# Where layer 1's own product is made, and which block layer 0 takes first

## The chip, the cores and the metric

The kernel runs on one core of one Trainium2 chip. The metric is the device time of one execution in microseconds. A core has five engines that run side by side and wait for one another by semaphores: TensorE (PE, matrix products and transposes, with its weight loads shown apart as PEld), VectorE (DVE), ScalarE (ACT), GpSimd (POOL) and SyncE (SP). In this kernel GpSimd issues the gathers and SyncE most plain transfers; sixteen DMA engines move the data.

## The reference

Four graph layers on N = 3327 nodes with D = 512 features. Each is `x = layernorm(x + layer(x, adj))`. `adj` is sparse (about 0.24% of the pairs times a weight that falls with the node number, so the first rows have by far the most neighbours).

```python
# layer 0: attention with 8 heads of 64
Wh = einsum('nd,hdo->hno', x, W);  f1, f2 = Wh.a1, Wh.a2
e = where(adj > 0, leaky_relu(f1[:, :, None] + f2[:, None, :]), -9e15)
x = layernorm(x + elu(softmax(e) @ Wh))
# layer 1: mean of the neighbours
agg = (adj > 0) @ x / max(deg, 1)
out = concat([x @ W_self + b_self, agg @ W_nb + b_nb]) @ W_comb + b_comb
x = layernorm(x + relu(out))
# layer 2: mean of the first 64 neighbours, its own weights
x = layernorm(x + leaky_relu(x @ W_line.T + b) + leaky_relu(mean64 @ W_nb.T + b))
# layer 3: attention with 4 heads of 128
```

Layer 1's output before the relu is linear in x. The kernel therefore makes two fused weights, `wx = W_self @ W_comb[:D]` and `wn = W_nb @ W_comb[D:]`, so that a node needs `x @ wx` ("own part", or self part, called z) and the mean over its neighbours of `x @ wn`.

## The kernel before

Nodes are worked on in NB = 26 blocks of 128. For each block an edge list is made first (on VectorE, from the adjacency rows); it says which table rows to gather. A chunk is 128 edges. Block 0 has three lists of 14 chunks; blocks 1 to 4 have 19, 15, 13 and 11 chunks, and later blocks from 10 down to 5. Up to four chunks form a group (one "item").

The edge lists are made by a generator, `structure`, that is advanced a step at a time between other work. The order of blocks is given here:

```python
LATE0 = 16
FIRST = 3
order = [*range(1, FIRST + 1), 0, *range(FIRST + 1, NB)]
...
def structure(big, mid, ps, m0):
    ...
    ms = masks(order[0], fetch(order[0]))       # ScalarE: adj -> 0/1; block 0's mask goes to m0
    yield None
    for k, b in enumerate(order):
        ab = fetch(order[k + 1]) if k + 1 < NB else None
        ...                                      # the list of block b
        yield k
```

Layer 0 first projects all blocks (`x @ W` into a table in HBM), then takes the items in the order of the blocks. The end of a block makes the new x, transposes it, multiplies by wn and stores the result as a row table for layer 1; for blocks below NB - LATE0 it also multiplies by wx:

```python
def layer0_end(b, acc):
    yield
    x1 = xres[b]
    e, mv, rs = yield from g0.summed(fin, acc, x1)
    scaled_by_act(x1, e, fin, mv, rs)
    xt = transposed(fin, ps, x1)                 # four 128x128 transposes, one copy
    yield
    tb = fin.tile([P, D], F32, name="tb", bufs=2)
    t3 = fin.tile([P, 3, D], BF16, name="t3", bufs=2)
    for _ in pieces(t3, tb, times(ps, xt, wn)):  # three bf16 pieces
        pass
    store(t1_d, b, t3.rearrange("p s d -> p (s d)"), 2)
    if b >= NB - LATE0:
        return
    yield
    zb = fin.tile([P, D], F32, name="tb", bufs=2)
    nc.scalar.copy(zb, times(ps, xt, wx))
    store(z1_d, b, zb)
...
for k, item in enumerate(groups(pools[0], order)):
    while ready < order.index(item[0]):
        more()                                   # one step of the lists
    work.add(g0.group(item, pools, accs, layer0))
    work.step()
    more(2 if k % 8 == 0 else 1)
```

Layer 1 takes block 0 densely (26 chunks in seven items, the adjacency row as weights) and the others through gathers of table rows into a ring. With each of the first LATE0 items one block's own part is made that layer 0 left out, with a transpose of its own:

```python
early = list(range(NB - LATE0, NB))
def self_part(b):
    yield
    xt = transposed(xts, ps, xres[b])            # the second transpose of x
    yield
    zb = fin.tile([P, D], F32, name="tb")
    nc.scalar.copy(zb, times(ps, xt, wx))
    store(z1_d, b, zb)
...
for items in (first_items(), groups(ring, range(1, NB))):
    for item in items:
        b, at = item[0], item[4]
        if at == 0:
            xin[b] = fin.tile([P, D], F32, name="zb", bufs=3)
            load(xin[b], z1_d, b)
        work.add(mean_group(item, t1_d, row0, lambda b, acc: ends.add(layer1_end(b, acc))))
        if early:
            ends.add(self_part(early.pop(0)))
        both()                                   # one step of all that is under way
```

`mean_group` gathers, makes a selection matrix, and adds up with three bf16 products per chunk. `layer1_end` adds z and the bias, normalises, transposes the new x and multiplies by layer 2's two weights (wn2 and wl2). The ring of layer 1 holds 15 + 4 chunks.

One more part is touched. From block 0's mask `m0` two transposed masks are made, one for all neighbours (row0) and one for the first 64 (near0). `near` has the place of the running count:

```python
zeros16 = lent(3 * D, BF16)
nc.gpsimd.memset(zeros16, 0.0)
...
so_far = lent(NP, I16)
nc.gpsimd.memset(rows[:, free:], 0.0)            # the rest of the ring
near = so_far.bitcast(BF16)
nc.vector.tensor_tensor_scan(so_far, m0, m0, 0.0, ALU.add, ALU.bypass)
for o in (row0, near0):
    if o is near0:
        nc.vector.scalar_tensor_tensor(near, so_far, KEEP, m0, ALU.is_le, ALU.mult)
    ...                                          # 26 transposes of m0 or near
```

Of the kernel before, what the change touches and what calls it, by code (L numbers as in the profile page):

```python
# [9 lines left out]
BF16 = mybir.dt.bfloat16  # L10
# [527 lines left out]
DENSE0 = 12  # L538
DENSE = 2
AHEAD = 2  # L540
LATE0 = 16

FIRST = 3
RING = 22 * 528
MORE = 3072
RANGE = 60.0
# [75 lines left out]
def sparse_path(ctx, tc, flag_i, x, adj, l0_w, l0_a1, l0_a2, l1_w_self, l1_b_self, l1_w_nb, l1_b_nb,  # L622
# [30 lines left out]
    dram = ctx.enter_context(tc.tile_pool(name="s_dram", bufs=1, space=DRAM))  # L653
    keep = pool_in(ctx, "s_keep")

    order = [*range(1, FIRST + 1), 0, *range(FIRST + 1, NB)]
    lists = []
    for b in range(NB):
        parts = HEAVY if b == 0 else ((0, SEGMENTS[b], CAPS[b], SLOTS[b], SEGMENTS[b], 1),)
# [168 lines left out]
    def structure(big, mid, ps, m0):  # L828
# [6 lines left out]
        def fetch(b):  # L835
            ab = abs_[b % len(abs_)]
            for s in range(2):
                w = min(HW, N - s * HW)
                if b == NB - 1:
                    nc.gpsimd.memset(ab[s][96:P, :], 0)  # L840
                for p0, p1 in rows_of(b):
                    nc.sync.dma_start(ab[s][p0:p1, :w], adj[b * P + p0:b * P + p1, s * HW:s * HW + w])
            return ab

        def masks(b, ab):
            ms = []
            for s in range(2):
                m = m0[:, s * HW:(s + 1) * HW] if b == 0 else big.tile([P, HW], BF16, name="m", bufs=2)
                nc.scalar.activation(m, ab[s], AF.Sign, accum_out=half[:, s, b:b + 1])  # L849
                ms.append(m)  # L850
            return ms

        ms = masks(order[0], fetch(order[0]))
        yield None
        for k, b in enumerate(order):
            ab = fetch(order[k + 1]) if k + 1 < NB else None
            val = big.tile([P, NP], U16, name="val")
            for s in range(2):
                nc.vector.tensor_mul(val[:, s * HW:(s + 1) * HW], ms[s], code[:, s * HW:(s + 1) * HW])
# [5 lines left out]
            for q, l in enumerate(lists[b]):  # L865
# [7 lines left out]
                for s in range(len(cuts) - 1):  # L873
                    seg = val[:, cuts[s]:cuts[s + 1]]
                    for r in range(rounds):
                        top = cand[:, s * rounds + r, :]
                        nc.vector.max(out=top, in_=seg)  # L877
                        if r + 1 < rounds:
                            nc.vector.match_replace(out=seg, in_to_replace=top, in_values=seg, imm_value=0.0)
                    if s == (len(cuts) - 1) // 2:  # L880
                        if q == 0 and ab is not None:
                            ms = masks(order[k + 1], ab)
                        yield None
                cf = cand.rearrange("p s e -> p (s e)")
                sl = mid.tile([P, K + 1], F32, name="sl")
# [34 lines left out]
                for c0 in range(0, L, G):  # L920
# [19 lines left out]
                    with nc.allow_low_precision(reason="whole numbers below 4096"):  # L940
                        nc.vector.tensor_reduce(l.idx[:, c0:c0 + g], eq, AX.X, ALU.add)
                    nc.vector.scalar_tensor_tensor(l.dst[:, c0:c0 + g], l.idx[:, c0:c0 + g], 0.0, v[:, :, 0],
                                                   ALU.is_gt, ALU.mult)
            yield k

    def groups(ring, blocks=range(NB)):

# [312 lines left out]
    with ExitStack() as pro:  # L1260
        wp = pool_in(pro, "l0pw", side="right")
        xp = pool_in(pro, "l0px", 2, side="right")
        ps3 = pool_in(pro, "l0pp3", 3, space=PSUM)
        ps2 = pool_in(pro, "l0pp2", 2, space=PSUM)
        ps1 = pool_in(pro, "l0pp1", 1, space=PSUM)

        ps = Banks(ps1, po=ps3, tr=ps2)
        banks = Banks(ps1, pv=ps2)
        m0 = lent(NP, BF16)
        made = structure(big, mid, banks, m0)  # L1270
        w0 = lent(DC * (D + 3 * H0)).rearrange("p (c s o) -> p c s o", c=DC, s=2)
        for c in range(DC):
            for s in range(2):
                nc.sync.dma_start(by_heads(w0, c, H0)[:, s],
                                  l0_w[s * H0 // 2:(s + 1) * H0 // 2, c * P:(c + 1) * P, :].rearrange("h p o -> p h o"))
        a0 = lent(2 * D).rearrange("p (s h o) -> p s h o", s=2, h=H0)
        for s, src in enumerate((l0_a1, l0_a2)):
            nc.sync.dma_start(a0[:, s].rearrange("p h o -> p (h o)"), row(src, H0 * OUT0))
        g0 = Gat("g0", t0_d, H0, OUT0, w0, 0)
        next(made)  # L1280
        score_weights(w0, xp, a0, H0, OUT0)

        def projection(b):
            load(xres[b], x, b)
            yield
            xt = transposed(xp, ps, xres[b], g0.xsum, b)
            yield
            pw = g0.products(ps, xt)
            yield
            g0.write(b, xp, pw)  # L1290

        def fused_weights():

            wc = lent(2 * DC * D).rearrange("p (c o) -> p c o", o=D)
            nc.sync.dma_start(wc, l1_w_comb.rearrange("(c p) o -> p c o", p=P))
            bc = wp.tile([P, D], F32, name="bcomb")
            nc.sync.dma_start(bc, row(l1_b_comb, D))
            bs = wp.tile([P, 2 * DC, 1], F32, name="bs")
            with nc.allow_non_contiguous_dma(reason="two small biases"):
                nc.sync.dma_start(bs[:, :DC, 0], l1_b_self.rearrange("(c p) -> p c", p=P))  # L1300
                nc.sync.dma_start(bs[:, DC:, 0], l1_b_nb.rearrange("(c p) -> p c", p=P))
            for s, (src, o) in enumerate(((l1_w_self, wx), (l1_w_nb, wn))):
                for i in range(DC):
                    raw = xp.tile([P, D], F32, name="raw")
                    nc.sync.dma_start(raw, src[i * P:(i + 1) * P, :])
                    yield
                    rt = transposed(xp, ps, raw)
                    yield
                    po = times(ps, rt, wc[:, s * DC:(s + 1) * DC, :])
                    nc.scalar.copy(o[:, i, :], po)  # L1310
            pb = ps.tile([P, D], F32, name="po")
            for k in range(2 * DC):
                bb = wp.tile([P, P], F32, name="bb", bufs=2)
                nc.vector.tensor_copy(bb, bs[:, k].to_broadcast([P, P]))
                nc.tensor.matmul(pb, bb, wc[:, k, :], start=k == 0, stop=k == 2 * DC - 1)
            nc.vector.tensor_add(bias1, pb, bc)

        def first_rows():

            zeros16 = lent(3 * D, BF16)  # L1320
            nc.gpsimd.memset(zeros16, 0.0)
            zero = zeros16[0:1, :]
            for r in range(2):
                nc.sync.dma_start(t1_d[r:r + 1, :], zero)
                nc.sync.dma_start(t2_d[r:r + 1, :], zero)
            so_far = lent(NP, I16)
            nc.gpsimd.memset(rows[:, free:], 0.0)
            near = so_far.bitcast(BF16)
            nc.vector.tensor_tensor_scan(so_far, m0, m0, 0.0, ALU.add, ALU.bypass)
            for o in (row0, near0):  # L1330
                if o is near0:
                    nc.vector.scalar_tensor_tensor(near, so_far, KEEP, m0, ALU.is_le, ALU.mult)
                for c0 in range(0, NB, 8):
                    g = min(8, NB - c0)
                    yield
                    pt = banks.tile([P, 8, P], BF16, name="lp")
                    for c in range(g):
                        src = m0 if o is row0 else near
                        nc.tensor.transpose(pt[:, c, :], src[:, (c0 + c) * P:(c0 + c + 1) * P], ident16)
                    nc.scalar.activation(o[:, c0:c0 + g, :], pt[:, :g, :], AF.Identity, saturate=False)  # L1340

        ready, whole = -1, True

        def more(n=1):
            nonlocal ready, whole
            for k in range(n):
                b = next(made, None)
                whole = b is not None or ready == NB - 1
                ready = ready if b is None else b

        fused = Stages()
        for t in range(NB):
            work.add(projection(t))
            work.step()
            more(3)
            if t == 4:
                fused.add(fused_weights())
            if t == 10:
                fused.add(first_rows())
            fused.step()  # L1360
        work.drain(more)
        fused.drain(more)
        g0.finish(xp, ps)
        while not whole:
            more()
# [42 lines left out]
                nc.scalar.copy(o[:, :, k * P:(k + 1) * P], pt)  # L1408

    w2lay = ExitStack()  # L1410
    for k, item in enumerate(groups(pools[0], order)):
        while ready < order.index(item[0]):
            more()
        work.add(g0.group(item, pools, accs, layer0))
        work.step()
        more(2 if k % 8 == 0 else 1)
        if ready == NB - 1 and wn2 is None:
            listlay.close()
            extra = pool_in(ctx, "s_more").tile([P, MORE], F32, name="gx")
            sp = pool_in(ctx, "s_sel", 3)  # L1420
            wp = pool_in(w2lay, "l2w")
            wn2 = wp.tile([P, DC, D], F32, name="wn2")
            wl2 = wp.tile([P, DC, D], F32, name="wl2")
            rawp = pool_in(lay, "l2raw", 2)
            work.add(transposed_weights())
# [322 lines left out]
```

## Time and profile before

| what | value |
|---|---|
| time, median of 3 runs | 1705.97 us (1705.8 to 1707.22) |
| profiled execution | 1704.1 us |
| PE, VectorE, ScalarE, GpSimd busy | 89%, 73%, 45%, 54% |
| moved by DMA | 410.17 MB, mean 241 GB/s |

Engines are busy side by side, so shares don't add up. A line of groups in the profile has the engine, the operation, its tiles with shapes, how often it occurs, busy time and mean of one, and then the idle time just before it with what ended that. A fp32 product of a block with a 512x512 weight is eight matmul records (four chunks of the weight, two records each); the transposes of a block are four. In time order the execution is: projection and first lists (to about 220 us), layer 0's blocks (to about 670), layer 1 (to about 1095), layer 2 (to about 1380), layer 3.

The matmuls of these parts on the page:

| group | records | busy us | mean ns |
|---|---|---|---|
| product with wx | 208 | 94.3 | 596 |
| product with wn or wn2 | 416 | 192.9 | 607 |
| transposes of x | 520 | 79.9 | 277 |
| layer 0's weighted sum | 1656 | 413.7 | 399 |

### The profile page before, as it was taken

The numbers are of one execution on the slowest core, as the hardware profiler recorded it, in microseconds if no ns is written. First come the engines' busy times: TensorE is split into PE (matmuls) and PEld (weight loads), VectorE is DVE, ScalarE is ACT, GpSimd is POOL, SyncE is SP. The second block draws the span as 40 slices with busy tenths as digits, with TensorE's granted clock in tenths as the row PEclk, the third lists the DMA queues.
The fourth block names the chain that finished last, engine by engine and source line by source line (L and its number), as shares of the span: only waits on it lengthen the run. The fifth ranks groups of instructions, "written<-read, shape, count | busy, mean of one in ns | idle before, by whom it ended". The sixth has DMA issues, their size and how long they took to land.

```text
span 1704.1 us, 25362 instructions
## 1 busy us (share of the span) xinstructions
PE 1523.7 (89%) x7947; PEld 981.5 (58%) x7947; DVE 1243.4 (73%) x3256; ACT 773.2 (45%) x2411; POOL 911.9 (54%) x1008
## 2 busy tenths in 40 slices
PE   5798958999999999999999999889989866998774
PEld 4565746777666664444444444446555545877653
DVE  8999988999998973124777884565434468798986
ACT  6557855667776764111111121122223222566664
POOL 2000067777666613646776552477777552677770
PEclk9999979999999999999999999999999987999997
DMA  8623687998775637978998776589999664677772
GB/s 300 233 100 107 207 288 237 313 309 266 258 231 176 179 90 282 317 237 272 341 328 296 246 241 241 204 279 317 318 312 322 234 227 157 189 230 224 227 220 74
DMA packets 121982, 410.17 MB, mean 241 GB/s; under 512 B 24768, under 2 KB 26304, under 8 KB 121838
## 3 DMA queue, kind: packets, MB, share of 16 engines
q0 software_dynamic: 69584, 286.13, 52.8%
q1 hardware_dynamic: 52254, 122.32, 20.4%
q8 instruction: 65, 1.06, 0.3%
q14 instruction: 79, 0.65, 0.1%
HBM read 360.34 MB, written 48.04 MB: 240 GB/s over the span
## 4 chain that ended last, share of the span: by engine, by line
PE 61%; DVE 16%; DMA 11%; ACT 6%; issue 3%; POOL 2%; SPq 0%; DVEq 0%; ACTq 0%; POOLq 0%
PE po L765 20%; PE acc L1196 15%; PE acc L1474 14%; DMA gt<-t_d,idx 7%; PE po L998 6%; PE pt L750 2%; DVE cand L877 2%; DVE gt L1188 2%; DMA gx<-t_d,idx 2%; POOL gt L966 2%; PE pg L1168 2%; DMA gd<-t_d 1%; DVE cand L891 1%; DVE sl L889 1%; ACT h L1213 1%
## 5 line engine op out<-in xcount | busy, mean ns | idle before, releaser
L966 POOL DMA_INDIRECT gt<-t_d,idx x739 | 742.1, 1004 | 578.9 <-DVE some L893 210.6
L1196 PE MATMUL acc<-gt,sel 128*128 128x264 f32 (+4 forms) x1656 | 413.7, 399 | 27.1 <-issue 20.1
L1196 PEld LDWEIGHTS acc<-gt,sel 128*128 128x128 f32 (+2 forms) x1656 | 311.4, 195 | 97.8 <-issue 42.9
L1188 DVE TENSOR_TENSOR gt<-gt,pg 128x1536 f32<-128x1536 f32 (+2 forms) x128 | 238.6, 1864 | 6.3 <-ACT gt L1181 2.9
L765 PE MATMUL po<-wn,xt 128*128 128x512 f32 x416 | 192.9, 607 | 3.8 <-ACT xt L753 3.8
L1474 PE MATMUL acc<-gt,sall 128*128 128x512 bf16 x489 | 117.3, 379 | 17.6 <-DMA gt<-t_d,idx 14.3
L765 PEld LDWEIGHTS po<-wn,xt 128*128 128x128 f32 x416 | 77.2, 193 | 89.4 <-issue 78.4
L966 POOL DMA_INDIRECT gx<-t_d,idx x107 | 107.6, 1006 | 38.6 <-issue 14.9
L877 DVE MAX8 cand<-val 128x8 f32<-128x832 uint16 (+38 forms) x259 | 125.7, 522 | 0.0
L1474 PEld LDWEIGHTS <-sall 128*128 128x128 fp8e4 x603 | 58.3, 97 | 98.4 <-issue 35.3
L1474 PE MATMUL acc<-gt,sel 128*128 128x512 bf16 (+3 forms) x486 | 113.3, 379 | 0.0
L998 PE MATMUL po<-gt,xt 128*128 128x268 f32 x416 | 106.0, 400 | 2.0 <-ACT xt L757 1.7
L1474 PEld LDWEIGHTS <-sel 128*128 128x128 bf16 (+3 forms) x603 | 57.9, 98 | 80.0 <-issue 22.7
L1156 ACT ACTIVATE far<-place,nmid 128x384 int16<-128x384 int16 (+3 forms) x137 | 86.9, 637 | 37.5 <-DVE ds L1160 34.5
L753 ACT COPY xt<-pt 128x512 f32<-128x512 f32 x86 | 50.8, 591 | 113.3 <-PE pt L750 113.2
L998 PE MATMUL po<-w,xt 128*128 128x262 f32 x416 | 96.2, 384 | 1.6 <-ACT xt L757 1.6
L765 PE MATMUL po<-wl,xt 128*128 128x512 f32 x208 | 94.0, 594 | 2.9 <-ACT xt L753 2.9
L765 PE MATMUL po<-wx,xt 128*128 128x512 f32 x208 | 94.3, 596 | 1.3 <-ACT xt L753 1.2
L750 PE MATMUL pt<-s_ident,xres 128*128 128x128 f32 x520 | 79.9, 277 | 17.4 <-DMA xres<-in_x_dram 16.6
L750 PEld LDWEIGHTS pt<-s_ident,xres 128*128 128x128 f32 x520 | 63.8, 143 | 46.2 <-issue 31.2
L1009 ACT COPY tg<-po 128x264 f32<-128x264 f32 (+1 forms) x104 | 39.9, 392 | 110.8 <-PE po L998 108.9
L849 ACT ACTIVATE m<-ab 128x1664 bf16<-128x1664 int32 x50 | 80.4, 1607 | 20.5 <-DMA ab<-in_adj_dram 15.6
(273 smaller groups left out, 2555.4 us busy)
## 6 DMA issues: line engine op xcount, KB each, us to landing
ab<-in_adj_dram SPq DMA_DIRECT2D x25, 832.0 KB
ab<-in_adj_dram SPq DMA_DIRECT2D x25, 831.5 KB
t_d<-t SPq DMA_DIRECT2D x50, 384.0 KB
gt<-t_d POOLq DMA_DIRECT2D x38, 384.0 KB, 7.8
gt<-t_d,idx POOLq DMA_INDIRECT x739, 4.8
t_d<-tg SPq DMA_DIRECT2D x25, 264.0 KB
t_d<-tg SPq DMA_DIRECT2D x25, 260.0 KB
gd<-t_d SPq DMA_DIRECT2D x25, 260.0 KB
```

The lines of the kernel that those rows point to most:

```text
L750: nc.tensor.transpose(pt[:, c, :], src[:, c * P:(c + 1) * P], ident)
L753: nc.scalar.copy(xt, pt)
L765: nc.tensor.matmul(po, xt[:, c, :], w[:, c], start=c == 0, stop=c == DC - 1)
L849: nc.scalar.activation(m, ab[s], AF.Sign, accum_out=half[:, s, b:b + 1])
L877: nc.vector.max(out=top, in_=seg)
L966: nc.gpsimd.indirect_dma_start(out=t[:m, c, :], out_offset=None, in_=table[:, :], in_offset=bass.IndirectOffsetOnAxis(ap=l.idx[:m, c0 + c: ...
L998: nc.tensor.matmul(pw[s], xt[:, c, :], self.w[:, c, s, :], start=c == 0, stop=c == DC - 1)
L1009: nc.scalar.copy(tb[:, s * hh:(s + 1) * hh, :], by_head[:, :, 1:])
L1156: nc.scalar.activation(far[:, :g * P], place[:, c0 * P:(c0 + g) * P], AF.Abs, bias=l.nmid, scale=2.0)
L1188: nc.vector.tensor_mul(Gc[:, :, :OUT], Gc[:, :, :OUT], w[:, :g].rearrange("p c (h o) -> p (c h) o", o=1).to_broadcast([P, g * H, OUT]))
L1196: nc.tensor.matmul(accs[b][s], S[:m, c, :], G[:m, c, s * hh * M:(s + 1) * hh * M], start=at + c == 0, stop=at + c == chunks_of[b] - 1)
L1474: nc.tensor.matmul(accs[b], S[:m, c, :], G[:m, c, k * D:(k + 1) * D], start=at + c + k == 0, stop=k == 2 and at + c == n - 1)
```

## The change

It does three things. LATE0 becomes 4, so the own part of all blocks but the last four is made at the end of layer 0's blocks, from the transposed x that is there, and twelve second transposes in layer 1 go. Layer 0 takes the blocks in plain order, block 0 first. And the mask for the first 64 neighbours is made in place of `m0`, without the memset of the ring's rest.

```diff
-LATE0 = 16
-
-FIRST = 3
+LATE0 = 4
...
-    order = [*range(1, FIRST + 1), 0, *range(FIRST + 1, NB)]
...
-        ms = masks(order[0], fetch(order[0]))
+        ms = masks(0, fetch(0))
         yield None
-        for k, b in enumerate(order):
-            ab = fetch(order[k + 1]) if k + 1 < NB else None
+        for b in range(NB):
+            ab = fetch(b + 1) if b + 1 < NB else None
...
-            yield k
+            yield b
...
-            zeros16 = lent(3 * D, BF16)
-            nc.gpsimd.memset(zeros16, 0.0)
-            zero = zeros16[0:1, :]
+            zero = lent(3 * D, BF16)[0:1, :]
+            nc.gpsimd.memset(zero, 0.0)
...
-            nc.gpsimd.memset(rows[:, free:], 0.0)
-            near = so_far.bitcast(BF16)
...
-                    nc.vector.scalar_tensor_tensor(near, so_far, KEEP, m0, ALU.is_le, ALU.mult)
+                    nc.vector.scalar_tensor_tensor(m0, so_far, KEEP, m0, ALU.is_le, ALU.mult)
...
-    for k, item in enumerate(groups(pools[0], order)):
-        while ready < order.index(item[0]):
+    for k, item in enumerate(groups(pools[0])):
+        b = item[0]
+        while ready < b:
             more()
```

More of the change, by code (lines that the diff above doesn't have):

```diff
@@ L881, in structure @@
                         if q == 0 and ab is not None:
-                            ms = masks(order[k + 1], ab)
+                            ms = masks(b + 1, ab)
                         yield None
@@ L1337, in first_rows @@
                     for c in range(g):
-                        src = m0 if o is row0 else near
-                        nc.tensor.transpose(pt[:, c, :], src[:, (c0 + c) * P:(c0 + c + 1) * P], ident16)
+                        nc.tensor.transpose(pt[:, c, :], m0[:, (c0 + c) * P:(c0 + c + 1) * P], ident16)
                     nc.scalar.activation(o[:, c0:c0 + g, :], pt[:, :g, :], AF.Identity, saturate=False)
```

## The prediction

> **What bounds the kernel now.** I read the page's engine totals and its 40 slices first, to see whether one engine bounds everything. None does by its total, but the matmul engine is full from the seventh slice on, after VectorE has been full:
>
> ```profile
> PE 1523.7 (89%) x7947; PEld 981.5 (58%) x7947; DVE 1243.4 (73%) x3256; ACT 773.2 (45%) x2411; POOL 911.9 (54%) x1008
> ...
> PE   5798958999999999999999999889989866998774
> ...
> DVE  8999988999998973124777884565434468798986
> ```
>
> So the change has to be read by stage. The table of stretches, cut where the timeline changes character, gives each engine's busy time (PE, weight loads, DVE, ACT, POOL), the granted clock, the DMA share and GB/s:
>
> ```profile
> 0.00:220.00 220.00, 179.33 (x1041) 128.48 (x1041) 206.02 (x778) 144.59 (x507) 9.12 (x27) 0.97 0.57 192
> 220.00:270.00 50.00, 30.66 (x264) 25.24 (x265) 38.58 (x100) 27.56 (x73) 37.97 (x39) 0.77 0.89 297
> 270.00:640.00 370.00, 364.12 (x2278) 258.77 (x2276) 336.99 (x843) 256.95 (x741) 229.73 (x253) 0.99 0.71 225
> 640.00:674.00 34.00, 30.66 (x115) 16.75 (x114) 12.05 (x28) 17.57 (x41) 13.10 (x26) 1.00 0.85 311
> 674.00:780.00 106.00, 106.00 (x381) 51.20 (x380) 20.27 (x39) 20.17 (x37) 52.48 (x57) 1.00 0.78 262
> 780.00:920.00 140.00, 140.00 (x508) 64.03 (x507) 99.23 (x200) 23.21 (x46) 105.36 (x102) 1.00 0.94 324
> 920.00:1015.00 95.00, 95.00 (x331) 42.61 (x330) 76.48 (x161) 19.19 (x37) 48.44 (x48) 1.00 0.75 240
> ```
>
> The reader is to see five things. To 220 us (projection of x, edge lists) VectorE is busy 206 of 220. From 220 to 270 (the first gathers of layer 0) nothing is full and PE works 31 of 50. From 270 to 640 (rest of layer 0's blocks) PE has 364 of 370, VectorE 337. From 674 to 1015 (layer 1) PE is busy all the time. Within it, DMA is nearly full only from 780 to 920.
>
> Busy PE could still hide waits, so I went on to the timeline of PE just after 674 us. Columns are start, length, engine, line, operation:
>
> ```profile
> 677.38 3.60 PE L765 MATMUL po<-wx,xt 128*128 128x512 f32 x8
> 680.82 0.60 PE L750 MATMUL pt<-s_ident,xres 128*128 128x128 f32 x4
> 681.25 2.75 PE L1474 MATMUL acc<-gt,row 128*128 128x512 bf16 x12
> 683.84 3.60 PE L765 MATMUL po<-wx,xt 128*128 128x512 f32 x8
> ```
>
> Each starts where the one before stops delivering. From start to start: a product with wx takes 680.82-677.38 = 3.44 us, four transposes 681.25-680.82 = 0.43 us, four chunks of layer 1's neighbour sum 683.84-681.25 = 2.59 us (0.65 a chunk). These pitches, not the busy times, are what I charge. Layer 1's first 106 us are thus one self part (3.87 us) plus one group, again and again, sixteen times; the product of a self part stays in layer 1 for blocks 10 to 25.
>
> Last, who waits on that stretch. The groups of 674 to 780 us show GpSimd's gathers waiting for PE, not the reverse:
>
> ```profile
> L966 POOL DMA_INDIRECT gt<-t_d,idx x40 | 38.6, 966 | 36.8 <-PE acc L1474 30.4 <-issue 6.1 <-DMA gt<-t_d 0.3
> ```
>
> 40 gathers there lost 30.4 us because their ring slots were still being read. Where they run free, the timeline of GpSimd gives the pitch:
>
> ```profile
> 787.01 0.95 POOL L966 DMA_INDIRECT gt<-t_d,idx  x1 [0.30 <-issue]
> 788.27 0.95 POOL L966 DMA_INDIRECT gt<-t_d,idx  x1 [0.31 <-issue]
> ```
>
> That is 0.95 busy and 0.30 of issue: 1.25 us a gather.
>
> **What the Trainium skill says.** "Perfetto Trace Analysis", section "Identifying the Most-Contended Engine", says that matmul busy share misjudges the distance to the limit because matmuls are pipelined. The trace agrees: the page has 596 ns busy for one wx matmul, eight of them would be 4.8 us, and the pitch is 3.44. The same page, "Optimization Strategy", says a kernel with several regimes can gain by interleaving them. The old kernel does this in layer 1: self parts, which need no table, lie beside the front of the gathers. "TensorE: Matmul & The Clock Gate", section "Part 4: PE-mode transpose", says a transpose goes to PSUM and must be copied out, and gives about 275 ns in a kernel's context. The page shows 277 ns busy, and 591 ns for ScalarE's copy of four; but four follow one another in 0.43 us, so the second transpose of x is cheap. "DMA: Bandwidth & Descriptors", section "Where 436 GB/s comes from", puts HBM's limit for one core at about 358 GB/s. Here a share of 0.94 goes with 324 GB/s, so about 324/0.94 = 345 is all there is.
>
> **The change part by part.**
>
> First, LATE0 goes from 16 to 4. Twelve blocks (10 to 21) get their own product at the end of their layer-0 block, from the transposed x that is still there. Removed in layer 1: 12 x (3.44 + 0.43) = 46.4 us of PE, and 12 copies of 0.59 us on ScalarE, which lie beside PE and count nothing. Added in layer 0: 12 x 3.44 = 41.3 us. The difference of the work alone is 12 x 0.43 = 5.2 us. Both places lie where PE is the bound, so each term counts almost fully.
>
> Not quite fully in layer 0: between 552 and 604 us PE shows waits of 0.38, 1.09, 0.83 and 2.46 us for VectorE or ScalarE, 4.8 together. Blocks 10 to 21 end about there, so I take 4 us back: layer 0 gets 37 us longer. The products share one PSUM bank with the lists' small matmuls, but the old kernel does the same for blocks 0 to 9 and shows no wait on PE from 290 to 540 us.
>
> Not quite fully in layer 1 either, which is the term I am least sure of. The chunks of blocks 1, 2, 3, 4 are 19, 15, 13, 11 (capacity over 128, rounded up). A block's end in layer 1 costs PE two products and a transpose, 2 x 3.44 + 0.43 = 7.3 us. Gathers against PE: block 1 19 x 1.25 = 23.8 against 19 x 0.65 + 7.3 = 19.7; block 2 18.8 against 17.1; block 3 16.3 against 15.8; block 4 13.8 against 14.5, and every later block is PE's. So gathers alone leave PE without work for 4.1 + 1.7 + 0.5 = 6.3 us, where before the self parts filled it. DMA is tight as well: 58 gathers of 0.393 MB, and four z loads of 0.262 and four stores of 0.393, are 25.4 MB; at 345 GB/s 73.7 us, against 72.5 us for 58 gathers. I add 4 us for the latency of a gather (median 5.4 us to landing) with no lead in the ring. Together 10 us, so layer 1 gets 46.4 - 10 = 36 us shorter.
>
> Second, the order: block 0 (42 chunks) first instead of after blocks 1 to 3 (47 chunks). Up to the first weighted table both kernels issue the same 671 VectorE instructions and the lists of the same number of blocks, so the first 220 us should stay. After that, 61 chunks instead of 41 pass in PE's order before the first block-end product. Without such products PE takes about 0.9 us a chunk for the sum and 0.24 for scores and transposes, near the 1.25 us of a gather. Ends are put off by 20 chunks or 25 us; two ends of 7.3 us that used to fill holes come later, on a full PE. In the old trace PE ran without gaps from 276 to 290 without any end, so most of it is no loss: 4 us.
>
> Third, the separate near tile goes, and with it a memset of the ring's rest on GpSimd, which is idle until 220 us: nothing. The mask is now overwritten in place, so VectorE's compare follows the transposes that read the mask; a few us at most, in a stage where it has other work queued: nothing.
>
> Sum: +41.3 - 4 - 46.4 + 10 + 4 = +4.9 us, or 1706 + 5 = 1711 us.
>
> **The rivals.** (A) Pure PE count: layer 1's ring hides the gathers, the order is free, and 5.2 us of transposes plus the filled gaps are gained: about 1697 to 1701 us. For it speaks that PE is full in both stages, and that items 5 to 7 and four self parts keep PE busy some 31 us after layer 0, while the first gathers land. (B) The front of layer 1 turns into a gather and DMA stage: PE waits for "DMA gt" 15 to 25 us, and layer 1 wins only half of what layer 0 pays: 1716 to 1726 us. For it speaks the DMA share of 0.94 from 780 to 920 with PE full; against it that gathers waited for PE 30 us in the stretch before. (C) The delayed ends of layer 0 leave PE idle like in 220 to 270 us, for 20 chunks more: 8 to 12 us above my sum. Against it speaks that PE was gapless from 276 on.
>
> **Range and chances.** The terms that can move are the front of layer 1 (2 to 20), the order (0 to 12) and the gaps filled in layer 0 (0 to 6). That gives 1697 to 1724 as a range for 8 in 10. The 2% borders are 1672 and 1740: the first would need six times the removed transposes, the second all rivals at once. Chances: faster 0.02, same 0.94, slower 0.04.
>
> **What would show it.** Layer 1's first product with wn should come some 37 to 41 us later, and the transposes of x should be 472 instead of 520. PE should have waits named "DMA gt" or "gx" in layer 1's first 80 us, some 10 us in sum; GpSimd's waits for "PE acc L1474" (line moved by three or so) should fall from 77 us in layer 1 to under 45. The end of layer 1's last gather, 1015 us now, should lie at 1014 to 1025. The first wn product of layer 0 should start later than 292.6 us, at about 310. It would be wrong if the first 220 us changed by more than 5 us, since I hold both orders equal there, or if layer 0 grew by clearly less than 35 us, which would mean that PE was not its bound.

## The result: 0.8% slower, and where in the execution it is lost

The changed kernel takes 1720.54 us (median; 1717.82 to 1724.19) against 1706.6 us of the old one. The ratio is 1.0082 with a 95% interval of 1.0062 to 1.0102, some 14 us. The profiled execution took 1715.8 us.

The table of stretches again, now of the changed kernel (busy PE, weight loads, DVE, ACT, POOL, then granted clock, DMA share, GB/s):

```profile
0.00:220.00 220.00, 180.39 (x1041) 129.88 (x1041) 205.82 (x775) 143.39 (x505) 8.87 (x26) 0.96 0.59 192
220.00:270.00 50.00, 32.68 (x257) 26.90 (x258) 35.87 (x92) 24.44 (x60) 37.39 (x38) 0.73 0.81 267
270.00:335.00 65.00, 54.65 (x390) 42.04 (x389) 52.67 (x126) 33.95 (x92) 44.12 (x48) 0.92 0.83 268
335.00:640.00 305.00, 301.33 (x1745) 202.77 (x1744) 263.11 (x676) 210.89 (x606) 176.66 (x196) 0.99 0.68 215
674.00:780.00 106.00, 103.53 (x408) 52.76 (x407) 37.71 (x77) 32.83 (x76) 51.44 (x67) 1.00 0.80 282
780.00:920.00 140.00, 137.74 (x487) 62.24 (x487) 92.66 (x186) 21.01 (x41) 107.59 (x107) 0.96 0.95 332
```

For the third stretch, which the first table did not have on its own, the old kernel answers:

```profile
270.00:335.00 65.00, 64.35 (x434) 48.01 (x432) 60.55 (x143) 40.16 (x107) 50.19 (x53) 0.98 0.84 263
```

The reader is to see that the engines' work in the first 220 us is the same, and that 270 to 335 us lost 9.7 us of busy PE (64.35 to 54.65) and a further 4 us of clock (0.98 to 0.92 of 65 us).

Three marks in PE's timeline split the execution: the end of layer 0's last product with wn, the end of the last product of layer 1, and the end. All values are in us.

| | layer 0 ends | layer 1 takes | the rest |
|---|---|---|---|
| before | 669.2 | 428.2 | 606.7 |
| after | 719.8 | 390.7 | 605.3 |

Layer 0 is 50.6 us longer and layer 1 37.5 us shorter. The prediction had +41 and -36. The other 10 us are in layer 0, and the timeline of VectorE around the end of block 0 shows most of them. Columns are start, length, engine, line, operation and, in brackets, the idle time before it with what ended it; changed kernel:

```profile
308.46 0.18 DVE L769 BATCH_NORM_AGGREGATE mv<-st 128x2 f32<-128x6 f32 x1
...
311.45 0.18 DVE L914 TENSOR_TENSOR dl<-p,dl 128x25 bf16<-128x25 f32 x1 [0.24 <-ACT dl L913]
319.97 0.16 DVE L821 SCALAR_TENSOR_TENSOR nm<-mv,rs 128x1 f32<-128x1 f32 x1 [8.33 <-POOL rs L778]
```

And GpSimd's timeline of the same time:

```profile
316.93 0.94 POOL L963 DMA_INDIRECT gt<-t_d,idx  x1 [0.30 <-issue]
317.95 0.18 POOL L777 TENSOR_SCALAR rs<-mv 128x1 f32<-128x1 f32 x1
318.40 0.91 POOL L963 DMA_INDIRECT gt<-t_d,idx  x1 [0.27 <-issue]
319.34 0.59 POOL L778 TENSOR_TENSOR rs<-rs,s_mhalf 128x1 f32<-128x1 f32 x1
```

The mean and variance (mv) of block 0 are ready at 308.6 us. The root (rs) is two tiny instructions on GpSimd, but in GpSimd's order it stands behind a row of gathers at 1.25 us each and runs only at 319.3. VectorE has placed the use of rs (nm) ahead of the next groups' work, and waits 8.33 us for it in order. With VectorE stopped, nothing prepares a group, and PE stops too:

```profile
321.97 1.12 PE L747 MATMUL pt<-s_ident,xres 128*128 128x128 f32 x4 [5.56 <-ACT xres L822]
...
324.24 5.18 PE L1193 MATMUL acc<-gt,sel 128*128 128x264 f32 x12
```

Twelve such matmuls take 2.89 us elsewhere in this stretch and 5.18 here: the granted clock is at half from 321.7 to 328.6 us, and was so once before the hole, from 311.5 to 314.9.

In the old kernel block 1's end comes first:

```profile
279.24 0.17 DVE L772 BATCH_NORM_AGGREGATE mv<-st 128x2 f32<-128x6 f32 x1
...
287.54 0.58 POOL L781 TENSOR_TENSOR rs<-rs,s_mhalf 128x1 f32<-128x1 f32 x1
...
288.15 0.16 DVE L824 SCALAR_TENSOR_TENSOR nm<-mv,rs 128x1 f32<-128x1 f32 x1
```

Its root is hardly quicker: from mv to the end of the second instruction it takes 8.7 us, against 11.3 in the changed kernel. But VectorE is kept busy until 288.07 us by work placed in front of nm, and nm runs without a wait. In the changed kernel this work ends 3.0 us after mv. So the two kernels differ in what stands in front of nm on VectorE, more than in GpSimd's delay.

### The profile page after: what moved, and what is told of

Read it like the earlier page. It is cut to its first block, busy times and chain, and to the rows that moved or that the text cites. A ratio compares the mean times of both kernels' runs of the same rounds, so it can differ in the third digit from the quotient of the medians.

```text
span 1715.8 us, 25248 instructions
## 1 busy us (share of the span) xinstructions
PE 1532.5 (89%) x7899; PEld 981.2 (57%) x7899; DVE 1246.6 (73%) x3260; ACT 770.7 (45%) x2403; POOL 907.9 (53%) x1007
## 5 line engine op out<-in xcount | busy, mean ns | idle before, releaser
L1193 PE MATMUL acc<-gt,sel 128*128 128x264 f32 (+4 forms) x1656 | 417.9, 401 | 21.4 <-issue 13.3
L1193 PEld LDWEIGHTS acc<-gt,sel 128*128 128x128 f32 (+2 forms) x1656 | 313.4, 196 | 93.5 <-issue 37.5
L1185 DVE TENSOR_TENSOR gt<-gt,pg 128x1536 f32<-128x1536 f32 (+3 forms) x129 | 238.9, 1852 | 9.7 <-ACT sel L1180 6.0
L874 DVE MAX8 cand<-val 128x8 f32<-128x832 uint16 (+39 forms) x259 | 126.2, 523 | 0.1
L750 ACT COPY xt<-pt 128x512 f32<-128x512 f32 x74 | 43.7, 590 | 114.1 <-PE pt L747 114.0
L747 PE MATMUL pt<-s_ident,xres 128*128 128x128 f32 x472 | 72.2, 278 | 21.9 <-DMA xres<-in_x_dram 16.3
L995 PEld LDWEIGHTS po<-gt,xt 128*128 128x128 f32 x416 | 76.8, 194 | 24.9 <-ACT xt L754 7.4
L995 PEld LDWEIGHTS po<-w,xt 128*128 128x128 f32 x416 | 79.8, 192 | 17.4 <-ACT xt L754 2.3
```

What stands on the lines that cost most here:

```text
L747: nc.tensor.transpose(pt[:, c, :], src[:, c * P:(c + 1) * P], ident)
L750: nc.scalar.copy(xt, pt)
L995: nc.tensor.matmul(pw[s], xt[:, c, :], self.w[:, c, s, :], start=c == 0, stop=c == DC - 1)
L1185: nc.vector.tensor_mul(Gc[:, :, :OUT], Gc[:, :, :OUT], w[:, :g].rearrange("p c (h o) -> p (c h) o", o=1).to_broadcast([P, g * H, OUT]))
L1193: nc.tensor.matmul(accs[b][s], S[:m, c, :], G[:m, c, s * hh * M:(s + 1) * hh * M], start=at + c == 0, stop=at + c == chunks_of[b] - 1)
```

## The experiments

Layer 0 is ordered by the automatic scheduler, so that a small edit moves many instructions. Every verdict below is therefore read from a whole time and from the marks, not from one alone. Ratios are to the old kernel.

**The order and the own parts apart.** order_only is the changed kernel with LATE0 back, so that it still holds the mask in place; late_only is the old one with LATE0 = 4.

```diff
-LATE0 = 4
+LATE0 = 16
```

> The changed kernel with LATE0 back at 16: only the block order (and the mask made in place) differ from the old kernel. Theory O (the loss is the order; moving the own parts is neutral, since layer 0 pays 12 x 3.44 = 41 us and layer 1 gives back 38.5): 1716 to 1721 us, nearly the whole loss of 14. Rival L (moving the own parts costs it, because layer 1 gives back less than layer 0 pays): 1705 to 1709 us. With O, layer 0's first product with wn starts near 329 us as in the changed kernel, and 61 chunks are summed by about 329 us without any product.

Measured: ratio 1.0086 (1.0073 to 1.0099), the whole loss.

```diff
-LATE0 = 16
+LATE0 = 4
```

> The old kernel with LATE0 = 4: only the own parts are moved, the order stays 1, 2, 3, 0. Theory O: 1703 to 1709 us (41.3 us more in layer 0, about 38 to 43 less in layer 1). Rival L: 1716 to 1721 us. PE's waits for gathers at the front of layer 1 should be there under both: 4 us or so in sum, and a drop of the granted clock behind them.

Measured: ratio 1.0038 (1.0023 to 1.0053) in six executions that lay between 1706.8 and 1716.4 us. Its profile took only 1704.7.

> late_only once more, for a second profile: its six runs lay between 1706.8 and 1716.4 us, and the profile was of the shortest, with 10 us of waits in layer 1 but no drop of the granted clock there. If the spread is the clock after those waits, a longer run shows half clock for 5 to 15 us between 700 and 900 us, as the changed kernel does at 782 us. If its clock there is full, the spread lies elsewhere.

The second profile took 1705.2 us, so it is not of a longer execution. It shows full clock from 674 to 1015 us, which can't settle the guess.

> late_only timed once more, since its six timed executions said 1.0038 while both of its profiles (1704.7 and 1705.2 us) lie at the old kernel's. If moving all twelve own parts is neutral (layer 0 pays 35.7 us, layer 1 gives back 35.7): ratio 0.998 to 1.002. If the exposed gathers of layer 1 cost what the profiles don't show: 1.003 to 1.005 again.

Measured: ratio 1.0022 (1.0012 to 1.0032) over 22 executions, between the two expectations. Moving all twelve own parts in the old order costs 0.2 to 0.4%, less in any case than the order.

The profile of this run is of a longer execution, 1711.8 us, and shows where the time went: 4.2 of the 7 us over late_only's first profile are in layer 0, 0.9 in layer 1. PE's waits for gathers are no longer than before (7.1 us from 680 to 1015 us, 7.6 in the first profile) and the clock there is full. In layer 0 the clock is at half from 580.6 to 584.0 and from 604.5 to 607.9 us, where late_only's first profile has full clock. Half of these 6.8 us, 3.4, is most of the 4.2. So neither expectation had the place.

The marks of the four kernels, with all three profiles of late_only:

| | layer 0 ends | layer 1 takes | profiled span |
|---|---|---|---|
| before | 669.2 | 428.2 | 1704.1 |
| late_only | 704.9 | 392.6 | 1704.7 |
| late_only (late_again) | 704.0 | 392.1 | 1705.2 |
| late_only (late_timed) | 709.1 | 393.4 | 1711.8 |
| order_only | 684.8 | 430.3 | 1720.2 |
| after | 719.8 | 390.7 | 1715.8 |

Moving the own parts costs layer 0 35.7 us in the old order (34.8 and 39.9 by the other two profiles) and 35.0 in the new one, and gives layer 1 back 35.7 (36.2 and 34.8) and 39.6. The order costs layer 0 15.6 us (after against the three of late_only: 14.9, 15.8 and 10.7) and gives nothing back. A mark of one execution is thus good to some 4 us. Theory O is right and rival L falls, save for the 0.2 to 0.4% that the own parts cost in the old order.

**The gathers at the front of layer 1.** PE's waits from 680 to 1015 us. In the second profile of late_only:

```profile
PE acc L1474 <- DMA gt<-t_d,idx: 5.0, 10, 1.3
PE acc L1474 <- DMA gx<-t_d,idx: 2.4, 5, 1.0
```

and in the changed kernel:

```profile
PE acc L1468 <- DMA gt<-t_d,idx: 3.9, 4, 1.6
...
PE acc L1468 <- DMA gx<-t_d,idx: 0.2, 1, 0.2
```

Columns are sum, number and longest in us. The old kernel has no such wait at all. On the other side, GpSimd's gathers in layer 1 waited for PE to free the ring 77.1 us before:

```profile
  PE acc L1474: 77.1, 76
```

and 38.6 us after:

```profile
  PE acc L1468: 38.6, 69
```

So with four self parts the gathers become the slower side for a while. late10 asks how many it takes to hide them:

```diff
-LATE0 = 16
+LATE0 = 10
```

> The old kernel with LATE0 = 10: six own parts are moved instead of twelve. Each saves 0.43 us of PE, so 2.6 us could be gained if the ten self parts left are enough to hide the first gathers of layer 1: 1703 to 1708 us, and no wait of PE for a gather in layer 1. If the gathers are exposed with ten as with four: 1707 to 1712 us.

Measured: 1703.96 us, ratio 0.9985 (0.9976 to 0.9995). Its profile has no wait of PE for a gather in layer 1. Layer 0 ends at 688.6 (+19.4 for six products of 3.44) and layer 1 takes 406.5 us (-21.7). This is the one version that is faster than the old kernel, by 2.6 us (0.9 to 4.1).

**The mask in place.**

```diff
-            near = so_far.bitcast(BF16)
...
-                    nc.vector.scalar_tensor_tensor(near, so_far, KEEP, m0, ALU.is_le, ALU.mult)
+                    nc.vector.scalar_tensor_tensor(m0, so_far, KEEP, m0, ALU.is_le, ALU.mult)
```

> The old kernel with only the near mask made in place of m0 (the memsets are kept): a null test. Both theories: within 2 us of the old kernel, 1704 to 1709 us. If it came out above 1712, the third part of the change would be part of the loss, and not the order.

Measured: ratio 1.0025 (1.0014 to 1.0036), 4.3 us, where nothing was expected: the edit removes no work, yet layer 0 ends at 673.7 instead of 669.2. PE and VectorE have the same work in another order. The trace shows what in that order costs the 4 us: at 388.0 us VectorE waits 3.32 us for a root, as in the changed kernel at block 0's end. PE stands still for 2.38 us, and the granted clock is at half from 392.4 to 395.8 us. Together this is 4.1 us.

**The order alone, without the mask.**

```diff
-FIRST = 3
+FIRST = 0
```

> The old kernel with FIRST = 0: the order becomes 0, 1, 2 ... and nothing else changes (the near mask keeps its place of its own, LATE0 stays 16). order_only held two changes, the order and the mask in place, and the mask alone gave 4 us. Theory O1 (the order alone is the loss): layer 0's last product with wn ends at 683 to 686 us against 669, and the whole is 1718 to 1723 us. Rival O2 (the two shares add, 4 of mask and 10 of order): 1713 to 1717 us.

Measured: 1727.81 us, ratio 1.0122 (1.0105 to 1.0139), above both ranges. Layer 0 ends at 688.4 (+19.2). VectorE's wait for the root is even longer here:

```profile
DVE nm L824 <- POOL rs L781: 11.3, 1, 11.3
```

The order alone is thus enough for the loss, and the shares of order and mask don't add: 1.0122 with the order, 1.0025 with the mask, 1.0086 with both. A part of first0's excess over order_only lies before the first chunk: its first weighted table starts at 235.8 us, that of order_only at 232.4.

**Block 0 second.**

```diff
-FIRST = 3
+FIRST = 1
```

> The old kernel with FIRST = 1: block 1 (19 chunks), then block 0 (42), then the rest. Theory O says that the loss comes from the first end of a block being late (after 61 chunks in PE's order instead of 41). Here block 1's end is early and supplies two products, but no other end comes until block 0 is through: 1707 to 1713 us, between the two kernels. If what counts were that block 0 is not first at all (its end the first to be reached), it would be like the old kernel, 1705 to 1708.

Measured: ratio 1.0044 (1.0032 to 1.0056); layer 0 ends at 678.6, between 669.2 and 688.4. The number fits theory O, but the trace doesn't. Layer 0's first weighted table starts at 240.1 us instead of 232.0, since VectorE is given 821 instructions (271.2 us busy) before it instead of 808 (265.9). Most of the 9.4 us is thus lost before the first chunk, and the run doesn't show what an early end is worth.

**Small blocks first.**

```diff
-    order = [*range(1, FIRST + 1), 0, *range(FIRST + 1, NB)]
+    order = [7, 8, 6, 1, 2, 3, 0, 4, 5, *range(9, NB)]
```

> The old kernel with the order 7, 8, 6, then 1, 2, 3, 0, 4, 5, 9 and on: three small blocks of 8 and 9 chunks first, so that the first products of an end come after about 30 chunks in PE's order instead of 41 (61 with block 0 first). If the time at which the first ends come sets the cost of the order, this gains: 1698 to 1706 us. If PE's holes between 220 and 270 us come from the first gathers' landing and VectorE alone, nothing can fill them and it stays at 1706 to 1712.

Measured: ratio 1.0029 (1.0018 to 1.0041), above both ranges. The first ends did come earlier (two wn products were done by the 42nd chunk, one in the old kernel), but they won nothing, and layer 0 ends at 676.6. The loss comes later: at 439.5 us VectorE waits 5.13 us for a root, PE stands still for 4.02 us, and the clock is at half from 442.5 to 445.9 us. So the time of the first ends doesn't set the cost of an order by itself.

**The hole at block 0's end.** after_gap puts two more steps between the root and its use, for every block of layer 0:

```diff
         nc.gpsimd.tensor_tensor(rs, rs, mhalf, ALU.pow)
-        yield
+        for _ in range(3):
+            yield
```

> The changed kernel with two more steps between GpSimd's root and VectorE's use of it at the end of layer 0's blocks. In the changed kernel VectorE waits 8.3 us for that root at the end of block 0, since it lies in GpSimd's queue behind gathers, and PE then idles 5.6 us and is granted half its clock for some 10 us. Theory H (this hole is a large part of the order's cost): the hole closes and 6 to 10 us come back, 1711 to 1715 us. Rival F (the cost is only that products to fill PE come late, the hole would otherwise be waited for elsewhere): 1718 to 1724 us, since the ends come later still.

Measured: 1718.71 us, ratio 1.0062 (1.0049 to 1.0076): 2 to 3 us won, within the noise. The hole is closed, and PE ends the 89th chunk at 359.8 us instead of 376.0, with two products fewer (6.9 us) made, so some 9 us ahead. But layer 0 ends at 718.7, only 1.1 us earlier. Counted like this, some 6 us of the lead are lost again between the 150th and the 200th chunk, and 3 more after the last chunk. There the last ends come two steps later and nothing is left to do beside them, which explains the second part at most; the first stays open. The old kernel with the same edit:

> The old kernel with the same two more steps. Its first ends show waits of VectorE for the root of at most 1.6 us, so theory H expects no gain: 1705 to 1712 us. Rival F expects a loss of up to 8 us, since each end's products come about two groups later while PE has holes: 1712 to 1717 us.

Measured: ratio 1.0041 (1.0027 to 1.0054). There is no hole to close at the first ends, and the edit costs 7 us, the number of rival F. But the products that come later are not the reason that the trace shows. The edit made a hole of the same kind at a later block. The second line is PE's:

```profile
410.74 0.16 DVE L825 SCALAR_TENSOR_TENSOR nm<-mv,rs 128x1 f32<-128x1 f32 x1 [7.41 <-POOL rs L781]
413.43 0.48 PE L929 MATMUL pv<-dl,u 128*128 128x26 bf16 x12 [6.48 <-DVE tb L814]
```

The clock is at half from 411.4 to 418.2 us. after_gap0 gives the two steps to block 0 alone:

```diff
         e, mv, rs = yield from g0.summed(fin, acc, x1)
+        if b == 0:
+            yield
+            yield
```

> The changed kernel with the two more steps at the end of block 0 alone. after_gap closed the hole (no wait of VectorE for the root up to 335 us, 8.6 us gained by the 89th chunk) but gave most of it back, since its last ends came two steps later with nothing left beside them. Theory H: here the hole closes and the ends of the other blocks stay, so 6 to 10 us of the loss come back: 1710 to 1715 us. If the order's cost is not in that hole (rival F): 1717 to 1723 us.

Measured: 1714.87 us, ratio 1.0051 (1.0032 to 1.0070), against 1.0082 for the changed kernel. VectorE of after_gap0, at the same place:

```profile
323.82 0.14 DVE L900 CAST dg<-dgs 128x1 bf16<-128x1 f32 x1
323.87 0.15 DVE L821 SCALAR_TENSOR_TENSOR nm<-mv,rs 128x1 f32<-128x1 f32 x1
```

No wait, though the root itself was no earlier (its second instruction ends at 319.0 us). The stretch from 270 to 335 us gets its work and its clock back:

```profile
270.00:335.00 65.00, 58.37 (x455) 46.13 (x454) 61.70 (x149) 40.94 (x118) 49.83 (x53) 1.00 0.88 285
```

VectorE has 61.70 busy instead of 52.67, PE works at full clock, and 455 instead of 390 matmuls go through. Layer 0 ends at 709.8, 10 us before the changed kernel.

The chunks of layer 0 show it best. Take the end of the n-th chunk's sum on PE, less 3.44 us for each product with wn or wx and 0.43 us for each block's transposes that are done by then. In the changed kernel the 61st chunk ends at 329.4 us, with no product and one block's transposes done; in the old one at 329.2, with four and two. So the changed kernel is 14.4 us behind there. In us behind the old kernel:

| | 42nd chunk | 61st | 89th | 150th |
|---|---|---|---|---|
| order_only | -2.2 | 13.5 | 14.6 | 15.0 |
| after | -1.0 | 14.4 | 15.6 | 16.0 |
| after_gap0 | -3.2 | 1.6 | 3.9 | 4.6 |
| first1 | 9.1 | 8.8 | 11.1 | 12.0 |
| small_first | -0.2 | 1.3 | 1.4 | 6.0 |
| inplace_only | 1.1 | 1.0 | 0.9 | 5.1 |

small_first and inplace_only lose between the 89th and the 150th chunk, where their holes are. What the order costs layer 0 arises between the 42nd and the 61st chunk, which is the place of its hole. after_gap0 passes this place with no product done either and loses 5 us there, not 15. So it was VectorE's wait, with the half clock around it, that cost the other 10, and not the lack of products.

In the whole time less of it is left. Layer 1 takes 394.7 us in after_gap0, 4 more than in the changed kernel: PE's waits in it are 7 us longer (16.7 against 10.0, for gathers and for copies by ScalarE), while the half clock that costs the changed kernel 5 us in layer 1 is not there. That makes 2 of the 4. The whole times differ by 5 to 6 us, and the intervals of the two ratios overlap. The hole is thus shown as the cause of 10 of the 15 us in layer 0. That closing it wins 5 us of the whole is likely, not shown. With the hole closed 1.0051 of the ratio remains, some 9 us; it was not divided between the own parts, the mask and the rest of the order.

## Why the prediction was right, and which term was not

The range (1697 to 1724) holds the 1720.5 us and the verdict "within 2%" is right. The middle was 9.5 us too low. There is some luck in it: the term of the order came out above the 0 to 12 us that the range allowed for it, and the other terms lay near their middles.

- **The own parts.** Predicted: layer 0 +37 (41.3 less 4 of filled gaps), layer 1 -36. Measured between order_only and after: +35.0 and -39.6; between before and late_only: +35.7 and -35.7. The pitches of 3.44 and 0.43 us from the timeline carried this, and the 472 transposes are there. The balance was put at +1 us; timed, it is 0.2 to 0.4% (4 to 6 us) in the old order, and within the noise in the new one.
- **The front of layer 1.** Predicted 10 us without work. PE waits 4.1 us for gathers in the changed kernel, and the granted clock is at half from 782.5 to 792.8 us, which costs 5 more. That makes about 9. (Nine matmuls of the sum take 4.11 us at 783.5 us and 2.11 at 777.3.) In late_only the waits are 7.1 to 7.6 us and the clock is full. So the size was right, but half of it in the changed kernel came from the clock, which the prediction did not have. GpSimd's wait for the ring fell to 38.6, under the 45 named. The 345 GB/s for a full DMA share was read from one stretch only; in the same table 640 to 674 us gives 311/0.85 = 366. Little rested on it (73.7 against 72.5 us).
- **The order.** This is the step that failed, by its size: "most of it is no loss: 4 us". It measured 15 us in layer 0 (15.6 by order_only, 14.9 between late_only and after). The step looked for the time at which products would fill PE, and saw that PE had run without gaps from 276 to 290 us with no end. What it left out is the first end's own chain through three engines in order: the root stood behind gathers on GpSimd, VectorE waited 8.33 us for it in front of its other work, PE idled 5.56 us, and 6.8 us of half clock followed. Rival C (8 to 12 us more) had the right 20 chunks and the right size, and PE was idle there; but its reason, that no products fill PE, falls with after_gap0, which has none there either. The first product with wn came at 329 us instead of the 310 named: that was the sign. The first 220 us were equal as held: the first weighted table starts at 233.7 us, and at 232.0 in the old kernel. The last product on a gather in layer 1 comes at 1038.8 us instead of 1025.5, 13 us later where the prediction had at most 10; this is the order's loss again.
- **The filled gaps of layer 0.** Predicted 4 us. late_only's three profiles have 34.8, 35.7 and 39.9 us for 41.3 us of products, so 6.5, 5.6 and 1.4 were filled: the size is right, and it depends on the execution. In the changed kernel it takes 324.0 us from the end of the 89th to that of the 243rd chunk, against 278.7. The 14 more products of 3.44 us are 48.2, so some 3 us were filled there too.
- **The mask.** Predicted nothing. In the old order it measured 4.3 us, most of it by the hole at 388 us that the shifted instructions made. With the order it made no such addition (1.0086 with it, 1.0122 without). Its share in this change can't be named.

Rival B (a front of 15 to 25 us) did not happen. Rival A (1697 to 1701 us) fell by the order, though without it late_only stands at 1710.3 us (late_timed) too; late10 shows that its idea holds for half of the move.

## What to carry to other kernels

When work is moved between two stages that one engine bounds, its pitch on that engine times the count tells both sides well. The gain is only what is not done twice. Ask then what the moved work had been hiding: here six of the twelve could go and four self parts were too few. And when the order of items changes, follow the first small chain through every engine's queue, not only the busiest one. Here a two-instruction root behind a row of gathers stopped VectorE, which feeds PE. In both orders the root took about as long; what counted was how much other work VectorE had been given before the use of it. Three small edits of the old kernel (inplace_only, small_first, before_gap) lost 4 to 7 us, each with such a hole at some later block. So when an edit that removes no work changes the time, look for a hole of this kind first.

## What the runs showed of the hardware that was not expected

After the 5.56 us hole at 316 to 322 us the granted clock was at half for 6.8 us, and twelve matmuls took 5.18 us instead of 2.89. So this hole was paid for a second time, with some 3.4 us. "TensorE: Matmul & The Clock Gate" of the Trainium skill, section "Why this matters for your kernels", says to avoid idle gaps over about 3 us between bursts, since the clock falls back. That fits this hole. But in the changed kernel half clock also came at 311.5 us, after a wait of 1.60 us, and at 782.5 us, in a wait of 1.64 us, while late_only's first profile had waits of up to 1.88 us in layer 1 and kept its clock. The rule does not tell these apart.
